# The convolution's partial sums in two PSUM buffers, added to the accumulator in two goes

## Chip, cores, metric

One NeuronCore of one Trainium2 chip. The metric is device time in microseconds, the median of three executions. The engines have short names below: PE is TensorE (matmuls), DVE is VectorE, ACT is ScalarE, POOL is GpSimd, SP issues the DMAs. PSUM is the memory that PE writes its sums to[...].

## What is computed

A network of two "metaformer" layers on an image batch x of shape (2, 96, 128, 128). Cut to what matters here:

```python
# layer 0
x = x + mamba_in_four_directions(ln_c(x))     # the scan, most of the time, not touched by the change
t = to_tokens(x)
t = t + ffn(ln_t(t), W1, b1, W2, b2)          # "ffn 0"
# layer 1
x = x + conv3x3(ln_c(x), kernel)              # (96, 96, 3, 3), padding 1
t = t + ffn(ln_t(t), W1, b1, W2, b2)          # "ffn 1"

def ffn(x, W1, b1, W2, b2):                   # operands rounded to fp8 (5, 2), sums to fp16 (5, 10)
    h = relu(q_acc(q_acc(q_mul(x) @ q_mul(W1).T) + q_mul(b1)))     # 96 -> 384
    return q_acc(q_acc(q_mul(h) @ q_mul(W2).T) + q_mul(b2))        # 384 -> 96
```

Each layernorm runs over the 96 channels, which lie on the partitions.

## The kernel before

For each of the two batch entries the kernel runs three stages one after the other: `normalize` (the layernorm ahead of the scan), `mamba` (the scan in two pairs of directions), and `ffn_and_conv`, which holds everything after it. The image, 96 channels on partitions by 16384 pixels, stays in SBUF as `acc` throughout.

`ffn_and_conv` is the stage that the change touches. It works in tiles of T = 512 pixels, four image rows, 32 tiles per batch entry. Four streams run in a software pipeline: in round r, ffn 0 takes tile r, `to_pad` (the layernorm ahead of the convolution, and the operands that it needs) tile r-1, the convolution tile r-3, and ffn 1 tile r-4. There are 36 rounds; rounds 4 to 31 hold all four streams. The instructions of each engine stand in the order in which the program emits them, and no scheduler moves them. The order within a round comes from `together` (L140): it goes through turns, and in each turn it takes every stream that has started one step further, up to its next `yield`, in the order ffn 0, ffn 1, to_pad, convolution. The table of stages (L634) gives each stream its lag in tiles and the turn in which it starts.

The steps of a layernorm (L121 to L138) are: PE centers the tile (xm, L124), ACT squares it (L127), PE takes the mean of the squares (v, L130), ACT takes Ln and Exp (L133, L134), DVE multiplies (L138). In ffn (L558 to L599) follow: two products "up" on PE (ph, L570), ACT's copies to fp16 (L574) with the third "up", DVE's bias and relu for two of the three blocks (L577, a cast to fp8 at L578), DVE's third relu and three products "po" on PE (L589), ACT's copy (L592), then DVE's bias add (L594) and POOL's add to `acc` (L595). For ffn 1 the tile is then stored to `out`. `to_pad` ends with DVE's L138 into a padded tile and with POOL's three combinations of neighbouring columns (L625, L627, L628) into `seg`, a buffer of eight tiles; at a segment's edge there is one more POOL copy (L630 or L632).

The convolution is done in pairs of columns: four combinations k of the inputs, each with three taps ky, so 12 products of 96x256 each, one per turn (each runs as two passes of the matrix engine, as every float32 product here does). Their sums lie in one PSUM tile of two banks, `pc`, of which there is one. When all 12 are done, four DVE adds bring them into `acc`:

```python
pc = psp.tile([C, 4, R * half_w], F32, name="pc", bufs=1)                              # L603
nc.vector.tensor_tensor(x, x, pc[:, 0:2, :], ALU.add)                                  # L611
nc.vector.tensor_tensor(x, x, pc[:, 2:3, :].broadcast_to((C, 2, R * half_w)), ALU.add) # L612
for k, op in enumerate((ALU.add, ALU.subtract)):
    nc.vector.tensor_tensor(x[:, k, :], x[:, k, :], pc[:, 3, :], op)                   # L614
```

A round, turn by turn, with c0 to c11 for the convolution's products: turn 0 xm of ffn 0; 1 its square; 2 its v, c0; 3 Ln and Exp, c1; 4 L138 of ffn 0, xm of ffn 1, c2; 5 the two ups of ffn 0, the square of ffn 1, c3; 6 L574, the third up, v of ffn 1, c4; 7 two relus of ffn 0, Ln and Exp of ffn 1, c5; 8 the third relu and po of ffn 0, L138 of ffn 1, xm of to_pad, c6; 9 L592 of ffn 0, two ups of ffn 1, the square of to_pad, c7; 10 L594 and L595 of ffn 0, L574 and third up of ffn 1, v of to_pad, c8; 11 two relus of ffn 1, Ln and Exp of to_pad, c9; 12 the third relu and po of ffn 1, L138 and POOL's combinations of to_pad, c10; 13 L592 of ffn 1, c11; 14 L594, L595 and the store of ffn 1, and the four adds. The next round follows with its turn 0.

Two dependences between the rounds matter: xm of ffn 1 (turn 4) reads the tile that the convolution's adds of the round before have written, and the products that use the lower neighbour rows (ky = 2) read what POOL wrote in the round before.

## Time and profile before

| what | value |
|---|---|
| median of three executions | 11283.08 us (11278.91 to 11287.82) |
| the profiled execution | 11287.49 us, its span 11285.7 us |
| mean granted TensorE clock | 0.984 |
| convolution's products (L608) | 1536 passes, 377/379/713 ns min/median/max |
| L608 waiting for the add at L614 | 50.2 us in 60 waits |
| L611, L612 (one each per tile) | 673 ns, 685 ns median |
| L614 (two per tile) | 414 ns median |

The profile is one execution taken by the hardware profiler. Times in it are microseconds from the first instruction. "Busy" of an engine is the time in which it has an instruction under way; matmuls overlap, so that one of 512 columns shows 0.59 us, though the next starts 0.43 us after it. The granted clock is what the throttle lets TensorE have, 1.00 being full speed. A chain of waits goes back from an instruction to what released it. L12 is line 12 of the kernel.

### The profile page before, as it was taken

What the parts mean: (1) busy time and instruction counts of PE and PEld (TensorE: products, weight loads), DVE (VectorE), ACT (ScalarE), POOL (GpSimd) and SP (SyncE); (2) the same over time, 40 slices, a digit from 0 to 9 for tenths busy, and PEclk for the clock granted to TensorE, in tenths of its full rate; (3) what the DMA queues carried; (4) which work ended last, traced back from release to release, by engine and by line L of the source; (5) the groups of instructions that cost most, each with busy time, mean ns of one, the idle gap of its engine ahead of it and who ended that gap; (6) DMA issues with size and microseconds to landing.
All of it is one profiled execution on the core that took longest, in us unless ns stands there. A gap on an engine that the chain in (4) does not pass through costs nothing.

```text
span 11285.7 us, 94221 instructions
## 1 busy us (share of the span) xinstructions
PE 10324.5 (91%) x24592; PEld 4019.4 (36%) x24592; DVE 10543.8 (93%) x10333; ACT 7902.4 (70%) x13564; POOL 9810.1 (87%) x4912
## 2 busy tenths in 40 slices
PE   8999999999999999988889999999999999999888
PEld 2333333333333333334433333333333333333344
DVE  6999999999999999995569999999999999999955
ACT  6777777777777777765567777777777777777655
POOL 5999999999999999992259999999999999999922
PEclk9999999999999999998989999999999999999988
DMA  7888888888888888880078888888888888888700
GB/s 278 344 337 339 342 340 341 337 340 340 337 340 341 338 338 345 336 319 18 27 261 342 339 337 344 337 337 344 337 340 342 340 342 336 340 342 336 312 13 13
DMA packets 540752, 3416.96 MB, mean 303 GB/s; under 512 B 67532, under 2 KB 68652, under 8 KB 143832
## 3 DMA queue, kind: packets, MB, share of 16 engines
q1 hardware_dynamic: 539960, 3410.16, 77.5%
q8 instruction: 199, 3.26, 0.1%
q14 instruction: 337, 2.76, 0.1%
q0 software_dynamic: 256, 0.79, 0.0%
HBM read 3289.04 MB, written 54.53 MB: 296 GB/s over the span
## 4 chain that ended last, share of the span: by engine, by line
DVE 56%; issue 19%; PE 11%; ACT 10%; POOL 2%; DMA 1%; DVEq 0%; SPq 0%; POOLq 0%; ACTq 0%
DVE da L355 34%; DVE row L355 10%; DVE row L450 9%; PE y L359 4%; ACT da L351 3%; PE pc L608 3%; POOL row L362 2%; ACT sz L261 2%; ACT L261 2%; PE xm L124 2%; ACT L262 2%; PE v L130 1%; PE ph L570 1%; DVE sz L366 1%; PE po L589 1%
## 5 line engine op out<-in xcount | busy, mean ns | idle before, releaser
L341 POOL TENSOR_TENSOR row<-dtu,row 128x2048 f32<-128x2048 f32 x1536 | 6951.3, 4526 | 8.9 <-DMA row<-bcd 8.3
L359 PE MATMUL y<-row,ident 128*128 128x512 f32 x12288 | 5681.4, 602 | 370.2 <-DVE row L450 357.5
L355 DVE TENSOR_TENSOR_SCAN da<-da,row 128x512 f32<-128x512 f32 x4608 | 5498.2, 1216 | 79.0 <-POOL row L362 22.5
L351 ACT ACTIVATE da<-dt,amat 128x512 f32<-128x512 f32 x6144 | 4234.6, 691 | 176.4 <-DVE row L355 6.3
L359 PEld LDWEIGHTS y<-row,ident 128*128 128x128 f32 x12288 | 2250.0, 190 | 3679.6 <-issue 2248.2
L450 DVE TENSOR_TENSOR row<-da,row 128x1024 f32<-128x1024 f32 x2304 | 2770.6, 1202 | 0.1
L362 POOL TENSOR_TENSOR row<-row,row 128x1024 f32<-128x1024 f32 x768 | 1807.0, 2353 | 268.7 <-issue 145.3
L451 ACT COPY hst<-da 128x2 f32<-128x2 f32 x2304 | 369.5, 160 | 2296.4 <-DVE row L450 2293.5
L355 DVE TENSOR_TENSOR_SCAN row<-da,row 128x512 f32<-128x512 f32 x1536 | 1847.8, 1203 | 71.0 <-POOL row L341 71.0
L213 PE MATMUL misc<-xa,inx 96*64 96x512 f32 (+1 forms) x2048 | 940.3, 601 | 25.4 <-DMA xa<-xnr 17.4
L213 PE MATMUL misc<-xb,inx 96*64 96x512 f32 (+1 forms) x2048 | 944.4, 604 | 18.6 <-ACT mix L249 13.6
L595 POOL TENSOR_TENSOR acc<-acc,y 96x512 f32<-96x512 f32 x128 | 147.2, 1150 | 599.1 <-DVE y L594 590.1
L374 PE MATMUL misc<-acc,ident 96*96 96x512 f32 x512 | 388.2, 843 | 218.5 <-ACT hst L451 196.5
L300 POOL TENSOR_TENSOR dtu<-dt,xc 128x512 f32<-128x512 f32 x384 | 487.8, 1270 | 91.2 <-DMA xb<-xnc 86.0
L213 PEld LDWEIGHTS misc<-xa,inx 96*64 96x64 f32 (+1 forms) x2048 | 324.6, 164 | 592.5 <-issue 484.5
L456 PE MATMUL y<-xc,dmat 128*128 128x512 f32 x768 | 420.7, 629 | 110.3 <-DVE sz L366 110.3
L608 PE MATMUL pc<-seg,uw 96*96 96x256 f32 x1536 | 443.7, 402 | 50.2 <-DVE acc L614 50.2
L376 PE MATMUL misc<-sz,gmat 128*96 128x512 f32 x1024 | 483.7, 594 | 0.0
L286 PE MATMUL misc<-rows,dtw 12*128 12x512 f32 x768 | 434.1, 645 | 50.6 <-ACT dt L291 37.9
L213 PEld LDWEIGHTS misc<-xb,inx 96*64 96x64 f32 (+1 forms) x2048 | 326.4, 164 | 279.5 <-issue 203.3
L345 POOL TENSOR_TENSOR row<-row,enter 128x4 f32<-128x4 f32 x1488 | 298.2, 200 | 116.6
L608 PEld LDWEIGHTS pc<-seg,uw 96*96 96x96 f32 x1536 | 259.0, 172 | 317.9 <-issue 178.4
(90 smaller groups left out, 7599.3 us busy)
## 6 DMA issues: line engine op xcount, KB each, us to landing
row<-bcd SPq DMA_DIRECT2D x3072, 1024.0 KB, 7.4
xc<-mix SPq DMA_DIRECT2D x256, 128.0 KB, 4.8
sz<-mix SPq DMA_DIRECT2D x256, 128.0 KB, 4.9
xa<-xnr SPq DMA_DIRECT2D x124, 193.1 KB, 5.2
xb<-xnc SPq DMA_DIRECT2D x124, 193.1 KB, 5.5
bcd<-rows SPq DMA_DIRECT2D x128, 128.0 KB, 4.3
acc<-in_x_dram SPq DMA_DIRECT2D x16, 768.0 KB, 5.8
xnr<-xn SPq DMA_DIRECT2D x16, 768.0 KB, 4.3
```

Of the source, the lines that this page charges most:

```text
L213: nc.tensor.matmul(ps[rows, :], w(PAIRS[pi][d], k, lo, hi), src[d][:, k : k + T], **se)
L261: nc.scalar.activation(d[name], d[name], AF.Silu)
L286: nc.tensor.matmul(d["ps"], w, d["rows"][0 : 2 * RK, :], start=True, stop=True)
L300: nc.gpsimd.tensor_tensor(dtu, d["dt"][:, g, :], d["xc"][:, g, :], ALU.mult)
L341: nc.gpsimd.tensor_tensor(b, d["dtu"][g][:, None, :].broadcast_to((128, 4, T)), b, ALU.mult)
L351: nc.scalar.activation(da[:, j, :], d["dt"][:, g, :], AF.Exp, scale=amat[:, pi, g, s + j : s + j + 1])
L355: nc.vector.tensor_tensor_scan(h[:, j, :], da[:, j, :], b[:, j, :], 0.0, ALU.mult, ALU.add)
L359: nc.tensor.matmul(y, ident, c[:, j, :], start=False, stop=s + j == S - 1)
L362: nc.gpsimd.tensor_tensor(c, h, c, ALU.mult)
L376: nc.tensor.matmul(d["po"], gmat[:, pi, 2 * g - 2 + k, :], d["yg"][g - 1 + k], start=False, stop=k == 1)
L450: nc.vector.tensor_tensor(c, h, c, ALU.mult)
L608: nc.tensor.matmul(pc[:, k, :], uw[:, k, ky, :], rows, start=ky == 0, stop=ky == 2)
```

## The change

The four combinations are split into two PSUM tiles of one bank each, `pc0` (k = 0, 1) and `pc1` (k = 2, 3), together as large as `pc` was. The add that needs only the first two (before at L611) is issued when they are done, in the middle of the round, ahead of c6; the other three follow after c11. The convolution's stream starts at turn 1 and not at turn 2, so that c0 to c5 stand in turns 1 to 6, the first add and c6 in turn 7, c11 in turn 12, and the last three adds in turn 13. The arithmetic and the number of instructions are the same.

```diff
             def conv(r):
 
-                pc = psp.tile([C, 4, R * half_w], F32, name="pc", bufs=1)
                 seg, lo = segs[r // SEG], r % SEG * R
-                for k in range(4):
-                    for ky in range(3):
-                        rows = seg[:, k, lo + ky : lo + ky + R, :]
-                        nc.tensor.matmul(pc[:, k, :], uw[:, k, ky, :], rows, start=ky == 0, stop=ky == 2)
-                        yield
                 x = acc[:, r * T : (r + 1) * T].rearrange("c (n k) -> c k n", k=2)
-                nc.vector.tensor_tensor(x, x, pc[:, 0:2, :], ALU.add)
-                nc.vector.tensor_tensor(x, x, pc[:, 2:3, :].broadcast_to((C, 2, R * half_w)), ALU.add)
+
+                def products(name, k0):
+                    pc = psp.tile([C, 2, R * half_w], F32, name=name, bufs=1)
+                    for k in range(2):
+                        for ky in range(3):
+                            rows = seg[:, k0 + k, lo + ky : lo + ky + R, :]
+                            nc.tensor.matmul(pc[:, k, :], uw[:, k0 + k, ky, :], rows, start=ky == 0, stop=ky == 2)
+                            yield
+                    return pc
+
+                outer = yield from products("pc0", 0)
+                nc.vector.tensor_tensor(x, x, outer, ALU.add)
+                inner = yield from products("pc1", 2)
+                nc.vector.tensor_tensor(x, x, inner[:, 0:1, :].broadcast_to((C, 2, R * half_w)), ALU.add)
                 for k, op in enumerate((ALU.add, ALU.subtract)):
-                    nc.vector.tensor_tensor(x[:, k, :], x[:, k, :], pc[:, 3, :], op)
+                    nc.vector.tensor_tensor(x[:, k, :], x[:, k, :], inner[:, 1, :], op)
...
-            stages = ((0, 0, partial(ffn, 0)), (4, 4, partial(ffn, 1)), (1, 8, to_pad), (3, 2, conv))
+            stages = ((0, 0, partial(ffn, 0)), (4, 4, partial(ffn, 1)), (1, 8, to_pad), (3, 1, conv))
```

## The prediction, made before the changed kernel ran

> **What bounds the kernel now.** I read the page first, then the busy time by stage, then the chain of waits through one round, and last the granted clock window by window.

> ```profile
> PE 10324.5 (91%) x24592; PEld 4019.4 (36%) x24592; DVE 10543.8 (93%) x10333; ACT 7902.4 (70%) x13564; POOL 9810.1 (87%) x4912
> ...
> PEclk9999999999999999998989999999999999999988
> ```

> These shares are averages over stages, and most of the span (the scan) is not touched. The touched stage runs once per batch, in slices 19 and 20 and again in 39 and 40. By stretches (columns: stretch and length, busy time and count of PE, PEld, DVE, ACT, POOL, then clock, DMA share, GB/s), its middle and its end in batch 0, and its middle in batch 1:

> ```profile
> 5142.38:5580.18 437.80, 400.17 (x1344) 202.43 (x1342) 277.69 (x589) 284.06 (x476) 128.60 (x148) 0.96 0.09 24
> 5580.18:5641.65 61.47, 44.09 (x116) 21.38 (x116) 22.12 (x49) 18.41 (x31) 7.89 (x9) 0.77 0.10 26
> ...
> 10778.98:11221.07 442.09, 404.52 (x1344) 204.40 (x1342) 277.71 (x589) 284.12 (x476) 128.76 (x148) 0.95 0.04 13
> ```

> PE is busy 91% there and DVE 63%: PE bounds it, through an in-order queue with gaps. Note the clocks 0.96, 0.95 and 0.77. The stretches run from one L611 to the L611 28 rounds later; the timeline shows single rounds at 15.04 us when PE's clock is full and 16.7 us when it was halved. The chain of waits at a round's end (start, length, what):

> ```profile
> 5358.81 0.66 PE po L589 x3
> ...
> 5359.55 0.59 ACT y L592
> ...
> 5360.17 1.15 DVE y L594
> 5361.32 0.61 DVE acc L611
> ...
> 5361.95 0.70 DVE acc L612
> ...
> 5362.67 0.76 DVE acc L614 x2
> ...
> 5363.57 0.62 PE pc L608
> ```

> The chain leaves PE with the last product of ffn 1 (call its end E, 5359.48) and returns 4.09 us later: ACT's copy, DVE's bias add, four adds of the convolution, then the next round's first convolution product, which waits for the last reader of "pc". Between 5348.53 and 5359.48 the same chain holds nothing but PE (0.05 us of issue apart). The clock, in windows of 3.41 us:

> ```profile
> 5360.27:5363.68 3.41, 2.13 (x6) 0.45 (x5) 3.08 (x5) 1.27 (x2) 3.35 (x5) 1.00 0.00 0
> 5363.68:5367.10 3.42, 3.42 (x7) 1.72 (x8) 0.69 (x1) 0.64 (x2) 0.26 (x1) 0.50 0.65 161
> ...
> 5264.70:5268.11 3.41, 2.46 (x7) 0.65 (x5) 3.22 (x6) 1.13 (x3) 3.10 (x4) 1.00 0.00 0
> 5268.11:5271.52 3.41, 3.07 (x12) 1.84 (x13) 0.88 (x2) 2.13 (x4) 0.25 (x1) 1.00 0.20 58
> ```

> A window with PE busy 2.13 us (62%) is followed by one at half clock; one with 2.46 us (72%) is not. In 58 consecutive windows every half-clock window follows one of 2.11 to 2.13 us; one of 2.15 us had no such follower. So the gaps at the end of a round cost twice: once themselves, and in some rounds 1.7 us more.

> [...]L594 takes 0.35 us in ffn 0 and 1.15 in ffn 1, where POOL's L625 (1.04 us) starts 0.04 before it.[...]

> **Part 1, the end of a round.** With two buffers, the next round's first product needs only the first buffer, read half a round earlier: the wait for L614 goes. The stage starts one turn earlier, so PE's order after E is: c11 (the last of the convolution's products c0 to c11), xm', c0', v', c1', c2', xm of ffn 1, c3', up0' (primes: the next round; xm and v are the layernorm's two products, L124 and L130, up0 the first of ffn's, L570; Sq, Ln, Exp are ACT's between them). Before: c10, c11, xm', v', [wait] c0', c1', xm, c2', up0'. From the chain and timeline rows: c is 0.43 a pair, xm 0.86. c11 and xm' end at E+1.29; Sq' 0.03+0.59 gives 1.91; v' starts 1.97 (c0' lies in that gap, hence free) and with the 1.10 of the row ends 3.07; Ln and Exp (0.03+0.68+0.03+0.63) 4.44; the multiplication to xq 0.03+0.69, 5.16; up0' can start at 5.19. PE's own order gives 3.07+0.43+0.43+0.86+0.43=5.22, the same, so both are late together. The pair of up then ends near E+5.79; before it ended at 5351.33-5344.44=6.89. Gain A = 1.10 us. What is late next: ACT's layernorm, no longer DVE. The inner adds follow L138 (end E+0.57) and c11: 0.69+0.75, done at E+2.1, before xm of ffn 1 needs them at E+3.9. Behind them queue L594 (held by POOL perhaps to E+2.9) and POOL's L595 and the store to out, on which nothing of the next round waits. Bounds of A: 1.25 if the restart of v' costs nothing, 0.85 if c0' must wait for POOL's L625 (E+1.7) and v' behind it.

> **Part 2, the middle of a round.** The outer add is put into DVE's queue between the second and third relu of ffn 0, and waits for c5. The rows there:

> ```profile
> 5353.22 0.35 DVE L577 TENSOR_SCALAR h<-h,b 128x512 f16<-128x512 f16 x1
> ...
> 5353.60 0.43 DVE L578 CAST hq<-h 128x512 fp8e5<-128x512 f16 x1
> 5353.72 0.81 PE L589 MATMUL po<-hq,w 128*96 128x512 fp8e5 x3
> ```

> The third relu starts at 5353.22, ends in hq at 5354.03, and the third product of po starts at 5354.15: cover of 0.12 us only. With the add, DVE waits for c5 (end 5353.45), adds 0.67 to 5354.16, and the third hq is ready at 5354.9, so that product starts at 5354.92 and ends at 5355.35 instead of 5354.53. PE stands still: loss B = 0.82 us. Behind the relu on DVE waits the multiplication of ffn 1 (end 5355.6), needed by PE only at 5356.5. Bounds: 0.70 if DVE's instructions overlap more, 0.95 if c5 is seen later. Net of a full round: 1.10-0.82=0.28 us; 2 x 28 rounds give 16 us (from -6 to +31 with the bounds).

> **Part 3, the clock.** PE's gaps after the change are about 0.25 us before v' and 0.6 us before the third po, 7 us apart; the emptiest window is then about 80% busy, above the 62%. The half-clock windows of the middle should go: the two middles are 437.80 and 442.09 us against 28 x 15.04 = 421.1, so 16.7+21.0=38 us. Bounds 0 and 38.

> **Part 4, the last rounds.** Rounds 32 to 35 of a batch have no ffn 0. From E of round 31 to the end of y16 in round 35 the chain shows 5641.65-5578.42=63.2 and 11280.76-11219.31=61.5 us, since c0' waited for L614 through 3.2 us of idle PE and then ran at half clock. After: ffn 1 starts at E+2.13 once the inner adds are done (c11 to c2' lie before it). Round 32 by the rows above: xm 1.10, c3, c4, v to 4.95, Ln, Exp, multiplication to 7.04, up0 at 7.07, then 3.80 as in a full round: 10.9. Rounds 33 and 34 the same without to_pad: 10.8 each. Round 35, partly at half clock (its chain takes 11.7 in all at half clock): 12.4. Sum 44.9 against a mean of 62.4: gain 17.5 per batch, 35 in all; bounds 12 and 21 per batch[...].

> **Sum.** 16+38+35=89 us. The profiled execution has 11287.49 us (span 11285.7), 4.4 above the median 11283.08. 11287.5-89-4.4 = 11194.

> **Rivals.**
> *No stall in the middle:* the relus are covered after all, B=0: 56 x 0.82=46 more, 11148. For it: DVE idles 37% here. Against: 0.12 us of cover in the rows.
> *The clock stays:* [...]the last rounds keep half their half-clock windows: 38 and 9 us are not won, 11241. For it: gaps remain. Against: 0.6 us is less than half of the 1.29 us of gap[...].
> *Slower:* the earlier start runs c0' into POOL. The rows that c0' to c2' read border on those POOL writes from E+0.65 to E+2.9. If c0' is held to the end of L628, it starts at 2.95, v' behind it at 3.4, up0' at 6.6: A turns to -0.3, a round costs 1.1 more (+62 us), the 1.6 us gap halves the clock more often (for windows at random phase about 20 of 28 rounds against 10 to 13, +28), less 35 for the last rounds: +55, 11338. It decides once c0' is held beyond about E+2.4. For it: the first product of round 3 did wait for a POOL row. Against:

> ```profile
> 5130.73 0.61 POOL L628 TENSOR_TENSOR seg<-xp 96x256 f32<-96x256 f32 x1
> 5131.11 1.06 PE L608 MATMUL pc<-seg,uw 96*96 96x256 f32 x2
> ```

> There c0 started 0.23 us before L628 ended: products wait for regions, not for the whole segment.

> **How the numbers follow.** Forecast 11194, chance 0.73, own range 11172 to 11225; no stall 0.08; clock stays 0.13; slower 0.05; no change 0.01. The range 11165 to 11240 holds the forecast and nearly the clock rival. A measurement here tells about 0.2% (23 us) from no change. Faster 0.93, same 0.02, slower 0.05.

> **What would show it.** Right: no wait of L608 for an add; c0 between xm and v; PE waiting for hq L578 before the third po in ffn 0, 0.6 us or more; rounds of 14.76 us; clock 1.00 in the middle; the last rounds near 11 us. Wrong: L608 waiting for POOL's seg rows; windows of 0.50 after busy ones; L594 or the inner adds delaying xm of ffn 1.

## The result, and the profile after

The changed kernel takes 11198.47 us (median of six, 11195.56 to 11201.95), the kernel before 11287.4 us beside it (also of six). The ratio is 0.9923, with a 95% interval of 0.9913 to 0.9933. The profiled execution's span went from 11285.7 to 11200.2 us, 85.5 us less. (In the profile of the changed kernel the convolution's products are L611, the add in the middle is L616, the two later ones L618 and L620, POOL's combinations L631, L633 and L634.)

By stretches, in the same columns as before: from the first add at the end of a round (now L618) to the same add 28 rounds later, then the last rounds, for batch 0 and for batch 1.

```profile
5142.97:5555.57 412.60, 386.17 (x1345) 197.98 (x1344) 255.33 (x589) 284.66 (x476) 127.48 (x146) 1.00 0.09 25
5555.57:5600.59 45.02, 35.20 (x116) 16.95 (x114) 21.21 (x49) 18.62 (x32) 9.01 (x10) 0.90 0.13 35
10737.38:11150.23 412.85, 386.36 (x1345) 198.07 (x1344) 255.53 (x589) 284.70 (x476) 127.46 (x146) 1.00 0.05 14
11150.23:11200.20 49.97, 35.19 (x116) 16.94 (x114) 21.55 (x50) 18.62 (x32) 10.15 (x11) 0.86 0.07 20
```

The two middles were 437.80 and 442.09 us and lose 25.2 and 29.2. The stretches behind them were 61.47 and 64.63 us (the latter from 11221.07 to the end of the span at 11285.7) and lose 16.5 and 14.7. The sum is 85.6, as much as the span lost, so nothing of note happened elsewhere. The clock in the middles is 1.00 instead of 0.96 and 0.95. PE is busy 93.6% there instead of 91%.

The chain of waits through the changed kernel, from the last products of ffn 1 in one round to the third po of ffn 0 in the next:

```profile
5332.99 0.65 PE po L589 x3
5333.64 0.43 PE pc L611 x2
5334.07 0.87 PE xm L124 x2
...
5334.97 0.60 ACT sq L127
...
5335.61 1.10 PE v L130 x2
5336.71 0.86 PE pc L611 x4
5337.58 0.86 PE xm L124 x2
5338.43 0.43 PE pc L611 x2
...
5338.87 0.59 PE ph L570 x2
...
5341.15 0.45 PE pc L611 x2
...
5341.62 0.68 DVE acc L616
5342.31 0.27 DVE h L577
...
5342.60 0.44 DVE hq L578
...
5343.08 0.38 PE po L589
```

At the round's end ACT's copy and the four DVE entries (L594 and the adds) are gone; one ACT entry, the square, is left between xm and v. In the middle there is now a piece of DVE that was not there: the first add, then the third relu and its cast, before the third po. Two lines from the waits of the whole stretch from 5142 to 5540 sum this up; no wait of L611 for an add is among them:

```profile
PE po L589 <- DVE hq L578: 17.1, 27, 0.7
...
PE v L130 <- ACT sq L127: 6.8, 27, 0.3
```

The first line is new (0.63 us in each of 27 rounds). The second stood at 19.1 us in 28 waits in the kernel before (its middle of batch 0, 5142 to 5580); c0 now fills most of that gap. The wait of L608 for L614, 16.2 us in 27 waits there, is gone.

### The profile page after: what moved, and what is told of

Its sections match the earlier page's. It is cut to its first block, busy times and chain, and to the rows that moved or that the text cites. A ratio compares the mean times of both kernels' runs of the same rounds, so it can differ in the third digit from the quotient of the medians.

```text
span 11200.2 us, 94163 instructions
## 1 busy us (share of the span) xinstructions
PE 10275.7 (92%) x24592; PEld 4000.7 (36%) x24592; DVE 10496.3 (94%) x10333; ACT 7927.2 (71%) x13564; POOL 9810.1 (88%) x4912
## 4 chain that ended last, share of the span: by engine, by line
DVE 55%; issue 18%; ACT 17%; PE 8%; DMA 1%; POOL 0%; DVEq 0%; SPq 0%; POOLq 0%; ACTq 0%
DVE da L355 33%; DVE row L355 10%; DVE row L450 9%; ACT da L351 5%; ACT L261 3%; ACT L262 3%; PE pc L611 2%; PE v L130 2%; PE xm L124 2%; ACT xc L261 2%; ACT sz L261 2%; PE ph L570 1%; DVE sz L366 1%; ACT xc L241 1%; ACT mix L249 1%
## 5 line engine op out<-in xcount | busy, mean ns | idle before, releaser
L213 PE MATMUL misc<-xa,inx 96*64 96x512 f32 (+1 forms) x2048 | 940.6, 601 | 24.1 <-DMA xa<-xnr 17.5
L213 PE MATMUL misc<-xb,inx 96*64 96x512 f32 (+1 forms) x2048 | 943.6, 603 | 19.5 <-ACT mix L249 14.7
L595 POOL TENSOR_TENSOR acc<-acc,y 96x512 f32<-96x512 f32 x128 | 147.1, 1149 | 524.5 <-DVE y L594 517.2
L611 PE MATMUL pc<-seg,uw 96*96 96x256 f32 x1536 | 424.8, 381 | 1.9 <-POOL seg L631 1.9
L268 PE MATMUL misc<-xc,bcw 128*96 128x512 f32 x768 | 355.7, 600 | 7.2 <-ACT xc L261 7.2
```

The lines of the kernel that those rows point to most:

```text
L213: nc.tensor.matmul(ps[rows, :], w(PAIRS[pi][d], k, lo, hi), src[d][:, k : k + T], **se)
L611: nc.tensor.matmul(pc[:, k, :], uw[:, k0 + k, ky, :], rows, start=ky == 0, stop=ky == 2)
```

## The experiments

Each ran beside the kernel before, and its time is a median; ratios are to the kernel before, with 95% intervals. The theory was the prediction's own: PE's in-order queue sets the round, a round's time is PE's work plus what PE waits for, and the half clock, which in the kernel before follows windows of 3.41 us with PE busy 2.11 to 2.13 us, goes when those windows are fuller.

### The clock alone

In the kernel before, a product whose result is overwritten was put into the gap before v of ffn 0; the arithmetic of the output is the same.

```diff
+        if fill:                       # 256 for ffn 0, otherwise 0
+            nc.tensor.matmul(v[:, 0:fill], mean_w, x[:, 0:fill], start=True, stop=True)
         nc.tensor.matmul(v, mean_w, sq, start=True, stop=True)
```

> The kernel before with one more product on PE in each layernorm of ffn 0: 256 columns of the tile times mean_w into the first half of v, which the real product v overwrites; it stands between xm' and v', in the gap of 0.68 us, and takes 0.43 us there. Theory[...]: rounds stay at 15.04 us and the waits stay, but the windows at a round's end are now about 75% busy, the clock is 1.00 in the middle of both batches, and the time falls by about 38 us to 11250. Rival (the clock drops for another reason, or more work on PE only costs): 11287 or more, clock 0.95 to 0.96 in the middle.

11247.34 us, ratio 0.9966 (0.9954 to 0.9979). The timeline at a round's end in this kernel, with the filler at L131, v at L132 and the convolution at L610:

```profile
5335.70 0.59 PE L131 MATMUL v<-acc,mean_w 96*96 96x256 f32 x2
...
5336.55 1.10 PE L132 MATMUL v<-sq,mean_w 96*96 96x512 f32 x2 [0.25 <-ACT sq L127]
...
5338.24 0.65 PE L610 MATMUL pc<-seg,uw 96*96 96x256 f32 x2 [0.60 <-DVE acc L616]
```

The wait for the last add is still there, 0.60 us as before, and the rounds are still 15.03 us long. From 5170 to 5550 and from 10810 to 11180 the clock is 1.00:

```profile
5170.00:5550.00 380.00, 356.59 (x1261) 185.20 (x1260) 250.91 (x531) 255.52 (x428) 118.16 (x136) 1.00 0.10 26
10810.00:11180.00 370.00, 345.35 (x1224) 179.73 (x1223) 243.82 (x516) 247.07 (x415) 115.00 (x132) 1.00 0.05 14
```

(the kernel before has 0.96 and 0.95 there). More work on PE made the kernel 38.8 us faster, against 38 expected. The clock's share of the gain is thus shown by itself, with no buffer changed.

### One buffer, started a turn earlier

The kernel before, with `(3, 2, conv)` changed to `(3, 1, conv)` and nothing else.

> The kernel before with one buffer of two banks, its convolution only started at turn 1. Theory: the four adds no longer stand behind L594 and end at E+2.7, but now c0' stands ahead of v' in PE's queue and waits for them, so v' starts at E+3.2 instead of 2.4, the pair of up ends at 6.9 to 7.1 as before, and the single gap of 1.4 us halves the clock at least as often. Rounds about 15.0 to 15.2 us at full clock, time 11275 to 11310. Rival (the earlier start alone wins): about 11230.

11323.64 us, ratio 1.0033 (1.002 to 1.0047): slower. The chain where two rounds meet:

```profile
5340.61 0.69 DVE xp L138
5341.30 0.61 DVE acc L611
...
5341.93 0.70 DVE acc L612
...
5342.65 0.76 DVE acc L614 x2
...
5343.55 0.64 PE pc L608 x2
5344.19 1.28 PE v L130 x2
```

The adds no longer stand behind L594, but c0 does stand ahead of v and waits for the last of them, 1.65 us on average (102.0 us in 62 waits). Rounds are 15.21 us at full clock, as expected, and 16.74 in most cases: the clock from 5170 to 5550 is 0.91. The time is 14 us above the range expected. In batch 1, from 10810 to 11180, the clock is 0.91 too, where the kernel before has 0.96 and 0.95: by an estimate from these shares (0.09 below 1.00 instead of 0.04 and 0.05), about twice as many windows ran at half clock. "At least as often" was right, but the range had not allowed for so many. So the start at turn 1 without the second buffer is worth less than nothing.

### Two buffers, started at turn 2, and where the first add stands

Five kernels vary the changed one in two things: the turn in which the convolution starts, and the product ahead of which the first add is issued. In this cut of the edit, LATE stands for a number, given with each kernel: the first add is issued so many products, one to a turn, later than in the changed kernel's code. The first of the five does without this edit.

```diff
-                def products(name, k0):
+                def products(name, k0, then=None):
...
+                            if then is not None and 3 * k + ky == LATE:
+                                nc.vector.tensor_tensor(x, x, then, ALU.add)
...
-                nc.vector.tensor_tensor(x, x, outer, ALU.add)
-                inner = yield from products("pc1", 2)
+                inner = yield from products("pc1", 2, outer)
```

> The two buffers, but the convolution starts at turn 2 as before. Theory: the first add then falls behind the third relu of ffn 0, so the middle costs nothing; c0' waits for no add; but v' follows xm' with no product between, so the gap of 0.68 us before v' stays and the pair of up ends near E+6.2 instead of 5.8 or 6.9. A round takes about 14.4 us, the gap of 0.68 us alone leaves a window 80% busy, so the clock stays at 1.00 in the middle, and the last rounds lose some 1.2 us each by L594 ahead of the adds. Time about 11180 to 11192, below the changed kernel. Rival (it is the earlier start that wins, the split only makes room for it): slower than the changed kernel, 11230 or more.

This one has the changed kernel's code with `(3, 2, conv)`. 11206.68 us, ratio 0.9929 (0.9914 to 0.9944). The sign was wrong: no better than the changed kernel, 8 us more by the medians, with rounds of 14.69 us and not 14.4. Its rounds are even a little shorter than the changed kernel's 14.75; what it loses are the last rounds (12.12, 12.88 and 11.25 us in batch 0, where the changed kernel has 11.05, 10.92 and 10.76). The rival's 11230 isn't met either. Together with the kernel of the section above, it shows which half of the change carries the gain: the second buffer without the earlier start gives about nine tenths of it (though its first add also stands elsewhere in DVE's queue), the earlier start without the second buffer gives nothing.

> The changed kernel, with only its first add moved on DVE by one turn: it is issued behind the third relu of ffn 0 and the multiplication of ffn 1, and before c7. Theory (PE's in-order queue sets the round; the add in the middle costs 0.82 us because the third po waits for the relu behind it): the wait of po for the cast L578 goes, a round takes about 13.9 us instead of 14.75, 56 full rounds give 46 us, the time is about 11152. Rival (ACT's layernorms set the round, and PE would only wait elsewhere for what it no longer waits for in the middle): rounds stay at 14.6 to 14.75 and the time at 11190 to 11198.

LATE = 1, start at turn 1. 11173.93 us, ratio 0.99 (0.9886 to 0.9915): 24.5 us below the changed kernel, where 46 were expected and none by the rival. Rounds are 14.25 us, not 13.9. The wait in ffn 0 is gone, but the chain has a new DVE piece in ffn 1. The timeline there (the add is L611, po and up as before):

```profile
5339.03 0.67 DVE L611 TENSOR_TENSOR acc<-acc,pc 96x512 f32<-96x512 f32 x1
...
5339.62 0.34 DVE L594 TENSOR_SCALAR y<-y,b 96x512 f16<-96x512 f16 x1
...
5340.10 1.15 POOL L595 TENSOR_TENSOR acc<-acc,y 96x512 f32<-96x512 f32 x1 [6.37 <-PE ph L570]
...
5340.68 0.73 DVE L577 TENSOR_SCALAR h<-h,b 128x512 f16<-128x512 f16 x1 [0.72 <-ACT h L574]
...
5341.44 0.43 DVE L578 CAST hq<-h 128x512 fp8e5<-128x512 f16 x1
```

The first relu of ffn 1 takes 0.73 us where it takes 0.35 before. It ends at 5341.41, 0.16 us after POOL's L595 (5340.10+1.15). In the two middles of the kernel before, every L594 of ffn 1 (56 of them, 1.15 us in most rounds) ends 0.14 to 0.16 us after the L625 beside it, and L594 of ffn 0, with no POOL instruction beside it, takes 0.35 us. In the kernel started at turn 2 the same relu stands in the chain with 0.74 us (5329.70 to 5330.44). The explanation to be tested: the add pushes L594 of ffn 0 back, hence L595, and the relu does not end before L595 does, as L594 beside L625. Both kernels that missed have the add at this place. Two more kernels put it behind L594 to see if that is the cause; a third does so with a start at turn 0.

> The changed kernel with its first add three turns later, before c9: behind the third relu of ffn 0, the multiplication of ffn 1 and also the bias add L594 of ffn 0. Theory (the version one turn later lost 0.35 us a round because the add pushed L594 back, so POOL's L595 of ffn 0 was still running when the first relu of ffn 1 came[...]): L595 of ffn 0 ends before or with the start of that relu, which takes 0.35 us again and not 0.73, a round takes about 13.9 us, time 11152 to 11158. Rival (the relu is slow for another reason, ACT's copies for instance, or PE's queue has another gap of that size): rounds stay at 14.25 and the time at 11174.

LATE = 3, start at turn 1. 11156.96 us, ratio 0.9884 (0.9868 to 0.9901), rounds of 13.95 us:

```profile
5333.47 0.35 DVE L594 TENSOR_SCALAR y<-y,b 96x512 f16<-96x512 f16 x1
5333.74 0.68 DVE L611 TENSOR_TENSOR acc<-acc,pc 96x512 f32<-96x512 f32 x1
5333.97 1.15 POOL L595 TENSOR_TENSOR acc<-acc,y 96x512 f32<-96x512 f32 x1 [5.75 <-DVE y L594]
...
5334.93 0.35 DVE L577 TENSOR_SCALAR h<-h,b 128x512 f16<-128x512 f16 x1 [0.51 <-ACT h L574]
```

The add still stands ahead of the relu in DVE's queue; what has changed is that L594 and L595 come earlier. POOL is through at 5335.12, when the relu is more than half done, so that ending 0.16 us after POOL costs it nothing: it has its 0.35 us again. The add itself takes 0.68 us beside POOL, as long as without it, so it isn't held. It reads one operand from PSUM, and L594 and L577 read none from there; whether that is the reason was not tested.

> Two buffers, start at turn 2 as before the change, the first add behind L594 of ffn 0 (before c8). Theory: [...]the first relu of ffn 1 is at 0.35 us again, a round takes about 14.35 to 14.4 us instead of 14.69, time 11186 to 11190. Rival: rounds stay at 14.69, time 11206.

LATE = 2, start at turn 2. 11190.99 us, ratio 0.9915 (0.99 to 0.993), rounds of 14.39 us. That is 1 us above the range expected. The 0.3 us that were missing have come back, and no relu stands in the chain from 5330 to 5346, which had it with 0.74 us, so the longer relu beside L595 explains that miss.

> As the one before, and the convolution starts at turn 0, so that c0' and c1' both stand between xm' and v'. Theory: they take 0.86 us in the 0.68 us that v' waits for ACT's square, so v' starts 0.2 us later after xm' than it could, but one product less stands elsewhere: the gap of 0.25 us and the slow restart of v' go, a round takes about 13.65 to 13.7 us, time 11138 to 11145. Rival (up0' waits for ACT's layernorm, whose start moves with v', so nothing is won): time equal to that of the version started at turn 1.

LATE = 4, start at turn 0. 11134.4 us, ratio 0.9865 (0.985 to 0.9879), the fastest of all, 64 us below the changed kernel and 4 us below the range expected. Most rounds are 13.52 us, 0.15 less than expected, and their chain from po to po is PE alone. Its part around the end of ffn 1:

```profile
5380.19 0.65 PE po L589 x3
5380.84 0.86 PE xm L124 x2
...
5385.11 0.65 PE po L589 x3
5385.76 0.86 PE xm L124 x2
5386.63 0.86 PE pc L613 x4
5387.49 0.92 PE v L130 x2
```

With c0 and c1 between xm and v, v takes 0.92 us instead of the 1.10 of a start after idle PE. I had counted the gap (0.23 us: the 0.66 us from xm to v less c0's 0.43) and not all of the restart (0.18 us); together they make 0.41 of the 0.43 us between the two versions.

Here the end of the room is near. In three rounds of each batch, where POOL makes one more copy at a segment's edge (now L639), a product does wait for POOL's rows, and the round takes 14.37 us:

```profile
5334.24 1.10 PE L613 MATMUL pc<-seg,uw 96*96 96x256 f32 x4 [0.77 <-POOL seg L639]
```

## Why the prediction was right

It forecast 11194 us against 11198.5 measured. The whole difference lies in the kernel before: its median over six executions was 11287.4, where the forecast had started from 11283.08. The gain was forecast at 89 us and is 88.9 by the medians. To agree so closely is in part luck: in the profiles the spans differ by 85.5, and the part that falls short is the last rounds.

- *The end of a round.* From E to the end of the up pair: 5339.46-5333.64=5.82 us against 5.79 worked out, so A is 1.07 us. As worked out, two things are late together: the layernorm, ACT's work and then L138, is through at 5338.82, and PE's own queue gets to ph at 5338.86. The adds end 2.0 us after E, and in full rounds nothing waits for them. DVE's reading of one buffer beside PE's writing of the other, which no run had shown before, costs nothing that can be seen: L618 and L620 run from 5334.15 to 5335.61, c0 of the next round starts at 5334.77, and the adds take 0.67 us and 0.75 us for both halves, where L612 and L614 took 0.69 and 0.75.
- *The middle.* The third po ends at 5343.46; the first began at 5341.85, and three of them without a stall take 0.81 us in the kernel before, so it would have ended at 5342.66: B is 0.80 us against 0.82. The experiment confirms it from the other side: moving the add out of the way takes 0.80 us from every round (14.75 to 13.95). The rival without a stall falls here.
- *A full round* takes 14.75 us against 14.76.
- *The clock.* No halved window is left in either middle, and the emptiest window from 5165 to 5545 is 81% busy. 38 us were forecast; the two middles lose 54.4 together, of which 56 x 0.29=16 is the shorter round and 38 the rest; the filler gives 38.8 alone. The rival in which the clock stays falls. One reading behind this part was too simple: that half clock follows a window busy 2.13 us and not one of 2.15 us. In the two middles of the kernel before it follows 21 of the 26 windows busy 2.11 to 2.15 us (last section). The forecast could do without it, since the windows went from 62% to 81%.
- *The last rounds.* Rounds 32 to 34 take 11.04, 10.92 and 10.76 us against 10.9, 10.8, 10.8. From E of round 31 to the end of y16 in round 35, batch 0 takes 5600.59-5555.05=45.5 us against 44.9: gain 17.7 against 17.5. Batch 1 also takes 45.5 us, from 11149.71 to 11195.23, but its rounds were shorter before (61.5): gain 16.0. The sum is 33.7 against 35. The time is right, the wait only in half of these rounds: ffn 1 was to start once the inner adds are done. In rounds 34 and 35 it does wait for L620, but in rounds 32 and 33 the product ahead of it waits for POOL, and xm of ffn 1 starts 2.29 us after E instead of 2.13. This share was only read in the traces; no experiment isolates it.
- *The slower rival* named a real wait, in the wrong place. L611 and its weight loads wait for POOL's seg rows 7.6 us in 14 waits, all told. Eight of them, for L631, are at the start of rounds 32 and 33, where PE has no ffn 0 to do first and reaches the ky=2 product early. The other six are weight loads that wait 0.34 us for L638, one of POOL's copies at a segment's edge; in the full rounds no product itself waits. With the start at turn 0 some do. The wait in round 32:

```profile
5556.83 0.67 PE L611 MATMUL pc<-seg,uw 96*96 96x256 f32 x2 [0.48 <-POOL seg L631]
```

What the prediction left unseen is not in its sum but in its picture: it asked what POOL does to L594 alone, rightly found that harmless (0.55 us beside L633 in most rounds of the changed kernel), and did not ask about the relus. In the two middles of the changed kernel 333 of 336 relus take 0.34 or 0.35 us and three 0.58 to 0.62, but a relu of 0.73 or 0.74 us beside L595 came to decide two of the experiments.

## What to carry to other kernels

When a wait is taken from an engine's in-order queue, list the whole new order of that queue and of the queue that gets the moved instruction: here one add moved into a DVE queue with 0.12 us of slack gave back 0.80 of the 1.07 us won, and three turns later in the same round it cost nothing. Small gaps on PE cost twice here: two of 0.68 and 0.60 us in one window of 3.41 us were followed by a clock of 0.50 in 21 rounds of the kernel before, and a product that is thrown away made it 38.8 us faster. Work that is there anyway, as c0 here, can fill them, and the clock per window shows whether that is at stake. An add that waits for nobody still delayed a relu through POOL (0.73 us instead of 0.35), so here it belongs behind, not ahead of, the DVE instruction that POOL waits for.

## What the runs showed of the hardware

```profile
5276.22:5279.64 3.42, 1.88 (x6) 0.90 (x6) 1.98 (x5) 0.60 (x2) 3.05 (x4) 1.00 0.00 0
5279.64:5283.05 3.41, 3.41 (x7) 1.70 (x6) 0.69 (x1) 1.48 (x3) 0.00 (x0) 0.50 0.20 58
...
5293.29:5296.70 3.41, 1.87 (x8) 1.15 (x8) 1.69 (x4) 0.91 (x2) 2.73 (x4) 1.00 0.02 5
5296.70:5300.12 3.42, 3.39 (x13) 1.67 (x12) 1.25 (x3) 2.79 (x6) 0.00 (x0) 1.00 0.20 58
```

The kernel before has such windows too. This one is as idle as those that half clock follows, and its second gap ends at 5520.68, at the window's end:

```profile
5517.28:5520.69 3.41, 2.12 (x6) 0.44 (x4) 3.18 (x5) 1.18 (x2) 3.31 (x4) 1.00 0.00 0
5520.69:5524.10 3.41, 3.38 (x13) 1.96 (x14) 0.88 (x2) 2.12 (x5) 0.00 (x0) 1.00 0.20 58
```

In the two middles of the kernel before, 26 windows are busy between 2.11 and 2.15 us. After 21 of them the clock is 0.50, and in these both gaps lie at least 0.07 us inside the window. After five it is 1.00, and in these a gap begins or ends within 0.03 us of the window's edge. Why these five are not followed by half clock was not tested. Of the 16 windows busy 2.19 to 2.60 us none is.
